# Transposing the adjacency of 64 small graphs: TensorE transposes against block loads and one VectorE transpose

## The chip, the cores and the metric

The kernel runs on one core of one Trainium2 chip. The metric is device microseconds of one execution; the median of three runs counts. The engines are named as in the profile: PE (TensorE), whose weight loads are listed as PEld, DVE (VectorE), ACT (ScalarE), POOL (GpSimd) and SP (SyncE), whose queue issues every DMA of this kernel.

## What is computed

Sixty-four independent graphs, each with 256 nodes and 512 features, pass through four graph layers. Every layer normalizes, clips at zero, mixes the nodes by a form of the adjacency, projects by a 512x512 weight (the last layer by 512x1024), and adds to the residual stream. All is float32.

```
h = max(layernorm(x), 0);  Wh = h @ W0
    e = leaky_relu(Wh @ a[:512] + (Wh @ a[512:])^T)
    x = x + elu(softmax(where(adj > 0.5, e, NEG_INF), axis=1) @ Wh)
h = max(layernorm(x), 0)
    Ah = adj + I;  d = rsqrt(rowsum(Ah));  x = x + relu((d * Ah * d^T) @ h @ W1 + bias)
h = max(layernorm(x), 0);  x = x + relu((adj @ h) @ W2) * mask
h = max(layernorm(x), 0);  agg = (adj @ h) / max(rowsum(adj), eps)
    x = x + relu(concat(h, agg) @ W3^T)
```

On TensorE the mixing products want the adjacency with its column index on the partitions, that is A^T. All four layers use it: layer 0 through its mask, layer 1 with the identity added, layers 2 and 3 as it is (in layer 3 scaled by the row sums).

## The kernel before

**One graph.** `graph(b)` describes the work of one graph as a list of operations, each with an engine, an estimated duration, a function that issues the instructions, and the tiles it reads and writes. It loads `xs` (the residual stream, two chunks of 128 nodes, line 353) and `a_nat` (the adjacency as it lies in memory, line 355). `transpose_a` (line 512) turns the four 128x128 quarters of `a_nat` on PE into a PSUM bank `pa`, and ACT copies the bank to `aT` in SBUF (line 522). DVE sums the rows of `a_nat` into `deg` (line 527), from which `dh` and `rdeg` follow.

Each layer then has the same frame. `norm` makes statistics (DVE), the scale (POOL) and `h` (ACT). `aggregate` (line 410) multiplies `h` with a moving matrix, in two halves `pt`: with `e` in layer 0 (the softmax, lines 546 to 581), `ahT` in layer 1 (`aT` plus identity, made by POOL, line 606), `aT` in layers 2 and 3. `left_sums` (line 396) brings the result out of PSUM in quarters and sums of quarters, and `project` (line 434) multiplies these by the weights with seven block products in place of eight (Winograd's scheme), in the PSUM banks `pz`, `py` and `pv`. DVE and ACT collect the results (`c`) and add them to `xs`. In layer 3 the product with `h` itself needs `h` transposed: DVE turns it in 32x32 blocks (`hb`, line 681), and 16 DMAs of 32 KB put each block to its place (`hw`, line 686). The result is stored from `xs` (line 701).

**The order.** No graph runs alone. `Plan` takes the operations of all graphs, with a due time that grows by `APART` = 14 for each graph, and `place` (line 69) goes through an imagined execution: each engine takes the operation that can start first, ties going to urgent ones and then to the earlier due time. `emit` writes the instructions out in the order of these starts, and this order is fixed for every engine, SP included. The estimates are multiplied by `STRETCH` except for PE and DMA; `SPARE` is added to the time at which a PE operation counts as ready. The plan's times only set the order: the instructions run as soon as what they need is there and the instruction before them on their engine has gone.

**Buffers.** Tiles share slots by tag. The number of slots of a tag is in `buffers` (line 713): five `xs` and five `aT`, one `a_nat`, four slots `mva` for `e` and `ahT`, one `off` for the mask (and, at the start, for the two halves of the vector a), and eight PSUM banks. A tile takes a slot once the one before has been read for the last time.

**Start.** `logit_weights` (line 256) multiplies W0 by the two halves of a, eight DVE operations (line 273) that the softmax of every graph waits for. `weight` and `last_weight` load the weights; POOL forms their block sums (line 293), and PE transposes W3 (line 329).

Of the kernel before, what the change touches and what calls it, by code (L numbers as in the profile page):

```python
# [14 lines left out]
P = 128  # L15
Q = 32
# [4 lines left out]
NEG_INF = -9000000000000000.0  # L21
HOP = 0.25
APART = 14.0
STRETCH = 1.12
SPARE = 0.0

# [12 lines left out]
class Plan:  # L41
# [9 lines left out]
        self.ops, self.writer, self.readers = [], {}, {}  # L51

    def add(self, eng, us, fn, reads, writes, tiles, due, urgent):
        if eng not in ("PE", "DMA"):
            us *= STRETCH
        op = Op(eng, us, fn, tiles, due, urgent)
        for k in reads:
            op.deps |= self.writer.get(k, set())
        for k in writes:
            op.deps |= self.writer.get(k, set()) | self.readers.get(k, set())  # L60
        for k in reads:
            self.readers.setdefault(k, set()).add(op)
        for k in writes:
            self.writer[k] = {op}
            self.readers[k] = set()
        self.ops.append(op)
        return op

    def place(self, buffers):
# [31 lines left out]
        for _ in self.ops:  # L101
            choice = None
            for eng, ops in waiting.items():
                here = None
                for op in ops:
# [3 lines left out]
                    ready = max(op.ready, got[0])  # L109
                    spare = SPARE if eng == "PE" else 0.0  # L110
                    rank = (max(free[eng], ready + spare), not op.urgent, op.due, op.at)
# [37 lines left out]
def kernel(  # L149
# [21 lines left out]
    nc = tc.nc  # L171
    B, N, F = x.shape
    O = w0.shape[1]
    NC = N // P
# [8 lines left out]
    ps = ctx.enter_context(tc.tile_pool(name="ps", bufs=1, space=PSUM))  # L183
# [4 lines left out]
    class Tiles:  # L188
# [5 lines left out]
        def declare(self, name, shape, pool=None, tag=None):  # L194
            tag = pool or tag or name
            self.tiles[name] = Buffered(shape, tag, f"{name}_{self.name}")
# [17 lines left out]
        def op(self, eng, us, fn, reads=(), writes=(), urgent=False):  # L214


            if eng == "DMA":
                us = 2.0 + us / 150.0
            named = [k.split(".")[0] for k in list(reads) + list(writes)]
            tiles = [self.tiles[n] for n in dict.fromkeys(named) if n in self.tiles]  # L220
            mine = lambda ks: [k if k[0] == "=" else (self.name, k) for k in ks]

            def go():
                self.open = tiles
                fn(self)

            plan.add(eng, us, go, mine(reads), mine(writes), tiles, self.due, urgent)


    ident = const.tile([P, P], F32, name="ident")  # L230
# [114 lines left out]
    def graph(b):  # L345

        me = Tiles(str(b), APART * b)
        op, declare, together = me.op, me.declare, me.together
# [85 lines left out]
        def project(operands, l, keep, keep_us, total, last, also=[]):  # L434
# [44 lines left out]
            snap("z", 0, 1)  # L479
            product("y", A12, B21, True)  # L480
            add("y", 0, 0)
            product("z", S3, T3, False)
            snap("z", 1, 1)
            add("v", 1, 1)
            product("z", A22, T4N, False)
            last(f"pz{l}")
            product("v", S4, B22, False)
            add("v", 0, 1)

        def plain_keep(i, j):  # L490
# [16 lines left out]
            )  # L507


        declare("pa", [P, NC, N], "ps")  # L510

        def transpose_a(g):
            for m in range(NC):
                for c in range(NC):
                    nc.tensor.transpose(  # L515
                        g["pa"][:, m, c * P : (c + 1) * P],
                        g["a_nat"][:, c, m * P : (m + 1) * P], ident
                    )

        op("PE", 0.45, transpose_a, ["a_nat", "=ident"], ["pa"])  # L520
        declare("aT", [P, NC, N])
        op("ACT", 0.59, lambda g: nc.scalar.copy(g["aT"], g["pa"]), ["pa"], ["aT"], urgent=True)
        declare("deg", [P, NC])
        declare("dh", [P, NC])
        declare("rdeg", [P, NC])
# [152 lines left out]

        declare("hb", [P, NC, F])
        for c in range(NC):  # L680
            op("DVE", 0.65, lambda g, c=c: nc.vector.transpose(g["hb"][:, c, :], g["h3"][:, c, :]),
               [f"h3.{c}"], [f"hb.{c}"])
        declare("hw", [P, 7, FH, P])
        parts = [(a, q) for a in range(P // Q) for q in range(P // Q)]
# [26 lines left out]
    for b in range(B):  # L711
        graph(b)
    buffers = dict(
        xs=5, a_nat=1, aT=5, h=4, mva=4, xw=4, hw=1, c=3, off=1, junk=4, b12=1, ex256=2, ex512=2,
        wa_col=1, hb=1, ps=8,
    )
    for tag in ("stats", "mv", "rstd", "nb", "deg", "dh", "rdeg", "lg", "top", "den", "mask"):
        buffers[tag] = 6
# [34 lines left out]
```

## Time and profile before

| what | value |
|---|---|
| median of three runs | 2949.46 us (2948.93 to 2951.12) |
| the profiled execution | 2949.19 us |
| its span, first to last instruction | 2947.4 us |
| mean granted TensorE clock | 0.997 |
| PE, pa matmuls (line 515) | 256 of 273 ns (median) |
| ACT, copy pa to aT (line 522) | 64 of 586 ns |
| DVE, transpose to hb (line 681) | 128 of 711 ns (median) |
| POOL, ahT (line 606) | 64 of 1291 ns |
| SP, one hw DMA issue (line 686) | 609 ns (median, 585 to 1905), 2.0 us to landing |
| SP, one a_nat issue (line 355) | 374 ns (median, 368 to 900), 2.7 us to landing |
| time of DMA packets | 17.1% of 16 engines' span, 335600 packets |

The span is measured by the profiler in one execution, and the 1.8 us between it and the time of the same execution lie around it. Busy times of PE overlap, as matmuls are pipelined: the mean duration of a 128x256 matmul is 379 ns, while 16 of them start within 3.45 us of each other. A float32 product of the code is two matmuls of the trace, so it occupies 0.43 us of the queue.

### The profile page before, as it was taken

What the parts mean: (1) busy time and instruction counts of PE and PEld (TensorE: products, weight loads), DVE (VectorE), ACT (ScalarE), POOL (GpSimd) and SP (SyncE); (2) the same over time, 40 slices, a digit from 0 to 9 for tenths busy, and PEclk for the clock granted to TensorE, in tenths of its full rate; (3) what the DMA queues carried; (4) which work ended last, traced back from release to release, by engine and by line L of the source; (5) the groups of instructions that cost most, each with busy time, mean ns of one, the idle gap of its engine ahead of it and who ended that gap; (6) DMA issues with size and microseconds to landing.
All of it is one profiled execution on the core that took longest, in us unless ns stands there. A gap on an engine that the chain in (4) does not pass through costs nothing.

```text
span 2947.4 us, 41121 instructions
## 1 busy us (share of the span) xinstructions
PE 2893.6 (98%) x13608; PEld 2536.1 (86%) x13608; DVE 2164.2 (73%) x5520; ACT 1364.4 (46%) x2899; POOL 1017.5 (35%) x1374
## 2 busy tenths in 40 slices
PE   5999999999999999999999999999999999999997
PEld 4888888888888888888888888888888888888886
DVE  8867777777777777777777777777777777777763
ACT  4544444444444444444444444444444444444432
POOL 6433333333333333333333333333333333333321
PEclk9999999999999999999999999999999999999999
DMA  4011111211211111111112111121121111121111
GB/s 146 15 34 50 44 37 39 51 36 40 50 30 47 47 33 47 42 38 47 37 40 51 36 40 49 31 48 46 34 47 38 39 50 36 40 51 30 43 29 36
DMA packets 335810, 127.21 MB, mean 43 GB/s; under 512 B 281968, under 2 KB 301424, under 8 KB 335600
## 3 DMA queue, kind: packets, MB, share of 16 engines
q1 hardware_dynamic: 335600, 124.60, 17.1%
q8 instruction: 109, 1.79, 0.3%
q14 instruction: 101, 0.83, 0.1%
HBM read 57.41 MB, written 33.55 MB: 31 GB/s over the span
## 4 chain that ended last, share of the span: by engine, by line
PE 97%; DVE 2%; SPq 1%; DMA 1%; issue 0%; ACT 0%; DVEq 0%
PE pz L451 37%; PE pt L420 30%; PE pv L451 19%; PE py L451 9%; PE pa L515 1%; SPq L686 1%; PE pl L240 0%; PE pr L240 0%; DMA a_l<-in_L_gnn_a_dram 0%; DVE junk_l L273 0%; DVE junk L541 0%; DVE e L565 0%; DVE e L563 0%; DMA hw<-hb 0%; DVE xs L595 0%
## 5 line engine op out<-in xcount | busy, mean ns | idle before, releaser
L451 PE MATMUL pz<-wb,xw 128*128 128x256 f32 x4096 | 992.7, 379 | 1.5 <-DVE c L611 1.2
L451 PEld LDWEIGHTS pz<-wb,xw 128*128 128x128 f32 x4096 | 773.4, 190 | 104.7 <-DVE c L611 1.4
L392 POOL TENSOR_TENSOR xw<-xw 128x256 f32<-128x256 f32 x512 | 418.5, 834 | 522.9 <-DVE xw L388 419.7
L451 PE MATMUL pv<-wb,xw 128*128 128x256 f32 x2048 | 525.5, 379 | 2.8 <-DVE c L493 2.8
L420 PE MATMUL pt<-aT,h 128*128 128x256 f32 x2048 | 473.4, 379 | 0.0
L420 PEld LDWEIGHTS pt<-aT,h 128*128 128x128 f32 x2048 | 389.1, 190 | 52.9
L451 PEld LDWEIGHTS pv<-wb,xw 128*128 128x128 f32 x2048 | 384.9, 190 | 53.3 <-issue 3.2
L491 ACT COPY c<-pz 128x256 f32<-128x256 f32 x576 | 214.5, 372 | 407.4 <-PE pz L451 392.2
L382 ACT ACTIVATE h<-xs,nb,rstd 128x512 f32<-128x512 f32 x512 | 390.2, 809 | 17.7 <-DVE nb L378 11.5
L371 POOL TENSOR_SCALAR rstd<-mv 128x2 f32<-128x2 f32 x256 | 127.7, 499 | 683.4 <-DVE mv L369 631.5
L367 DVE BATCH_NORM_STATS2 stats<-xs 128x6 f32<-128x512 f32 x512 | 333.2, 681 | 5.4 <-DMA xs<-in_x_dram 5.1
L493 DVE TENSOR_TENSOR c<-pv,c 128x256 f32<-128x256 f32 x384 | 161.8, 421 | 220.3 <-PE pv L451 171.5
L451 PE MATMUL pz<-wb,hw 128*128 128x256 f32 x1024 | 264.3, 381 | 10.8 <-DMA hw<-hb 9.6
L405 DVE TENSOR_TENSOR xw<-pt,xw 128x256 f32<-128x256 f32 x256 | 108.0, 422 | 225.0 <-ACT xw L400 224.9
L451 PE MATMUL py<-wb,xw 128*128 128x256 f32 x1024 | 263.1, 379 | 0.4 <-ACT xw L400 0.4
L392 POOL TENSOR_TENSOR hw<-hw 128x256 f32<-128x256 f32 x128 | 99.6, 781 | 436.3 <-DVE hw L388 418.3
L420 PE MATMUL pt<-e,h 128*128 128x256 f32 x1024 | 235.3, 383 | 11.2 <-DVE e L578 11.2
L400 ACT COPY xw<-pt 128x512 f32<-128x512 f32 x256 | 150.0, 586 | 189.8 <-PE pt L420 182.6
L420 PE MATMUL pt<-ahT,h 128*128 128x256 f32 x1024 | 232.2, 379 | 1.2 <-ACT h L382 1.2
L420 PEld LDWEIGHTS pt<-e,h 128*128 128x128 f32 x1024 | 196.4, 192 | 39.4 <-ACT h L382 8.9
L541 DVE SCALAR_TENSOR_TENSOR junk<-h,wa 128x512 f32<-128x512 f32 x256 | 228.2, 912 | 0.0
L451 PEld LDWEIGHTS pz<-wb,hw 128*128 128x128 f32 x1024 | 190.0, 191 | 35.8 <-issue 10.4
(90 smaller groups left out, 3552.5 us busy)
## 6 DMA issues: line engine op xcount, KB each, us to landing
xs<-in_x_dram SPq DMA_DIRECT2D x64, 512.0 KB, 4.2
hw<-hb SPq DMA_DIRECT2D x1024, 32.0 KB, 2.0
out_dram<-xs SPq DMA_DIRECT2D x64, 512.0 KB, 2.8
a_nat<-in_adj_dram SPq DMA_DIRECT2D x64, 256.0 KB, 2.7
w3n_w<-in_L_gnn_W_dram SPq DMA_DIRECT2D x4, 512.0 KB, 4.3
wb<-in_L_gnn_kernel_dram SPq DMA_DIRECT2D x6, 256.0 KB, 7.0
w_l<-in_L_gnn_W_dram SPq DMA_DIRECT2D x4, 256.0 KB, 6.8
wb<-in_L_gnn_W_dram SPq DMA_DIRECT2D x3, 256.0 KB, 3.9
```

The lines of the kernel that those rows point to most:

```text
L367: op("DVE", 0.69, lambda g, c=c: nc.vector.bn_stats(g[st][:, c, :], g["xs"][:, c, :]), XS[2 * c : 2 * c + 2], [f"{st}.{c}"])
L371: op("POOL", 0.31, lambda g: nc.gpsimd.tensor_scalar_add(g[rs], g[mv][:, :, 1], EPS_LN), [f"{mv}.0", f"{mv}.1"], [rs])
L382: op("ACT", 0.81, lambda g, c=c: nc.scalar.activation(g[h][:, c, :], g["xs"][:, c, :], AF.Relu, bias=g[nb][:, c : c + 1], scale=g[rs][:, c ...
L392: op("POOL", 0.85, lambda g, i=i, o=o: nc.gpsimd.tensor_tensor(g[xw][:, o], g[xw][:, i], g[xw][:, S2], ALU.subtract), put(i, S2), put(o), ...
L400: op("ACT", 0.59, lambda g: nc.scalar.copy(g[xw][:, A12 : A22 + 1 : A22 - A12].rearrange("p h k n -> p k h n"), g[hi].rearrange("p k (h n) ...
L405: op("DVE", 0.43, lambda g: nc.vector.tensor_tensor(g[xw][:, S1], g[lo][:, :, P:], g[xw][:, A22], ALU.add), [lo] + put(A22), put(S1), urge ...
L420: nc.tensor.matmul(g[pt][:, kk, :], lhsT=g[h][:, c, k * P : (k + 1) * P], rhs=g[moving][:, c, :], start=(c == 0), stop=(c == NC - 1),)
L451: nc.tensor.matmul(g[t], lhsT=g[xw][:, left, k], rhs=wb[n_w][:, right, k], start=start and at == 0, stop=at == ends, skip_group_check=True,)
L491: return "ACT", lambda g, to, block: nc.scalar.copy(to, block)
L493: plain_total = (0.43, lambda g, i, to, block: nc.vector.tensor_tensor(to, block, to, ALU.add))
L515: nc.tensor.transpose(g["pa"][:, m, c * P : (c + 1) * P], g["a_nat"][:, c, m * P : (m + 1) * P], ident)
L541: op("DVE", 0.77, lambda g, j=j, c=c: nc.vector.scalar_tensor_tensor(g[f"junk{j}{c}"], g["h0"][:, c, :], 1.0, wa[:, j, :], ALU.mult, ALU.mult,
```

## The change

The adjacency is loaded twice. `a_nat` stays, for the row sums. Beside it, eight DMAs of 32 KB bring the same matrix into a new tile `ab`, in 32x32 blocks: each block is put where its transpose belongs in A^T, but itself not turned. One DVE instruction then turns all 64 blocks in place of their positions and writes `aT`. The PE transposes, the PSUM bank `pa` and the ACT copy are gone. Each DMA moves runs of 32 floats, 128 bytes, 256 of them.

Along with this the planner's constants and the slots change: `STRETCH` becomes a factor for each engine (DVE 1.1, ACT 1.15, POOL 1.06, before 1.12 for all three), `SPARE` goes from 0 to 0.15, the estimate of the hb transpose from 0.65 to 0.71, and the slots are xs 6 (5), mva 3 (4), off 2 (1), ex256 3 (2), ex512 1 (2) and a new tag ab with 1. So the order of all engines is planned anew.

```diff
-STRETCH = 1.12
-SPARE = 0.0
+STRETCH = {"DVE": 1.1, "ACT": 1.15, "POOL": 1.06, "PE": 1.0, "DMA": 1.0}
+SPARE = 0.15
...
-        if eng not in ("PE", "DMA"):
-            us *= STRETCH
+        us *= STRETCH[eng]
...
-        declare("pa", [P, NC, N], "ps")
-
-        def transpose_a(g):
-            for m in range(NC):
-                for c in range(NC):
-                    nc.tensor.transpose(
-                        g["pa"][:, m, c * P : (c + 1) * P],
-                        g["a_nat"][:, c, m * P : (m + 1) * P], ident
-                    )
-
-        op("PE", 0.45, transpose_a, ["a_nat", "=ident"], ["pa"])
+        declare("ab", [P, NC, N], tag="ab")
         declare("aT", [P, NC, N])
-        op("ACT", 0.59, lambda g: nc.scalar.copy(g["aT"], g["pa"]), ["pa"], ["aT"], urgent=True)
+        for q in range(P // Q):
+            rows = adj[b].rearrange("(i r) (c q j) -> q r c i j", r=Q, c=NC, j=Q)[q]
+            for c in range(NC):
+                op("DMA", 32, lambda g, q=q, c=c, rows=rows: nc.sync.dma_start(
+                    g["ab"][q * Q : (q + 1) * Q, c, :].rearrange("r (i j) -> r i j", j=Q),
+                    rows[:, c]), (), [f"ab.{q}{c}"])
+        op("DVE", 0.7, lambda g: nc.vector.transpose(g["aT"], g["ab"]),
+           [f"ab.{q}{c}" for q in range(P // Q) for c in range(NC)], ["aT"])
...
-            op("DVE", 0.65, lambda g, c=c: nc.vector.transpose(g["hb"][:, c, :], g["h3"][:, c, :]),
+            op("DVE", 0.71, lambda g, c=c: nc.vector.transpose(g["hb"][:, c, :], g["h3"][:, c, :]),
...
     buffers = dict(
-        xs=5, a_nat=1, aT=5, h=4, mva=4, xw=4, hw=1, c=3, off=1, junk=4, b12=1, ex256=2, ex512=2,
-        wa_col=1, hb=1, ps=8,
+        xs=6, a_nat=1, ab=1, aT=5, h=4, mva=3, xw=4, hw=1, c=3, off=2, junk=4, b12=1, ex256=3,
+        ex512=1, wa_col=1, hb=1, ps=8,
     )
```

## The prediction, made before the changed kernel had run

> **What bounds the kernel now.** I read, in this order: busy shares and slices of the page, the chain that ended last (shares, then its pieces in order of time), one stretch of TensorE's timeline, the busy time of the transposes (tile pa) by stretch, and TensorE's waits.
>
> ```profile
> PE 2893.6 (98%) x13608; PEld 2536.1 (86%) x13608; DVE 2164.2 (73%) x5520; ACT 1364.4 (46%) x2899; POOL 1017.5 (35%) x1374
> ...
> PE   5999999999999999999999999999999999999997
> ...
> DVE  8867777777777777777777777777777777777763
> ...
> PE 97%; DVE 2%; SPq 1%; DMA 1%; issue 0%; ACT 0%; DVEq 0%
> ```
>
> TensorE is full in every slice but the first and the last, and 97% of the chain runs on it; in the first slice DVE is the fuller one (8 against 5). Pieces of the chain, start and length in us, each the first 16 instructions of one period:
>
> ```profile
> 2672.55 3.45 PE pt L420 x16
> ...
> 2717.46 3.45 PE pt L420 x16
> ...
> 2762.38 3.45 PE pt L420 x16
> ...
> 2806.85 3.45 PE pt L420 x16
> ```
>
> The chain repeats per graph: 44.91, 44.92, then 44.47 us. The last period is the first in which no adjacency is transposed (the last pa matmul starts at 2760.4). So the trace itself holds a period without the removed work: 0.45 us shorter. The timeline agrees:
>
> ```profile
> 1502.54 0.60 PE L515 MATMUL pa<-ident,a_nat 128*128 128x128 f32 x4
> 1502.98 1.03 PE L451 MATMUL pz<-wb,hw 128*128 128x256 f32 x4
> ```
>
> The next matmul starts 0.44 us after pa began, with no idle bracket at either. Where pa stands (stretch; TensorE busy, instructions; weight load; ACT or clock):
>
> ```profile
> 0.00:92.00 92.00, 3.98 (x20) 3.05 (x20) 2.91 (x5) 0.98 0.37 120
> 92.00:350.00 258.00, 3.00 (x20) 2.44 (x20) 2.95 (x5) 1.00 0.15 35
> 350.00:2800.00 2450.00, 32.40 (x216) 26.96 (x216) 31.66 (x54) 1.00 0.17 42
> ```
>
> Five graphs' transposes fall into the fill (0 to 92 us), where TensorE waits anyway; 5 + 54 = 59 stand in the full part. TensorE's own waits sum to 36 us before 92, 2.2 us from 92 to 2800 and 10.3 us after (hw DMAs at the end). The largest of the fill:
>
> ```profile
> PE pt L420 <- DVE e L578: 10.8, 2, 8.6
> PE pw_l L240 <- DVE mv L369: 9.7, 1, 9.7
> ```
>
> The fill is set by DVE, at whose end the first product starts, at 33.73 us.
>
> **What the Trainium skill says.** "VectorE: DVE Perf Modes", The three transpose paths: DVE turns only independent 32x32 blocks and writes SBUF, TensorE turns 128x128 into PSUM. So the blocks must be loaded in their final grid. The trace agrees in kind: hb is turned by DVE in blocks at 711 ns for 128x512. "DMA: Bandwidth & Descriptors", Why small descriptors are slow (HBM only): short runs from HBM pay a fixed overhead each. The hw copies have 128-byte runs but go SBUF to SBUF, so no row here shows it. "SBUF — State Buffer", Who interferes with whom: DVE and GpSimd share a port pair that one holds alone. In the trace DVE's L565 takes 1.64 to 1.68 us beside a busy POOL in the first 50 us and 0.69 later, while the 128 block transposes stay within 668 and 715 ns: the added operation is of the kind that isn't slowed.
>
> **The change, part by part.**
>
> TensorE: 4 transposes a graph go, 0.44 us of the queue. In the full part 59 x 0.44 = 26.0 us come off the end; the five in the fill bring nothing.
>
> ACT: 64 copies of 586 ns go (37.5 us). ACT is 46% busy and ends no wait of weight on the chain: nothing. The PSUM bank of pa goes too; no TensorE wait for it is seen: nothing.
>
> DVE: 64 x 0.71 = 45 us come. From 350 to 2800 us DVE is busy 1817.7 of 2450 us, 33.3 us of a period; after, 34.0 of 44.47 (76%). Its idle time there ends mostly on TensorE, which hides the addition. If that cover were gone, it would cost 0.71 x 59 = 42 us at most, nothing at least. In the order of the changed program's instructions I followed the tightest point: the second half of e (L576) is preceded on DVE by the sums of pv, pz, py of layers 1 and 2. From the end of the pz of layer 1 DVE has hw's sum, one c sum, L576 and the pz sum itself, about 0.48 + 0.42 + 0.42 + 0.35, with hops about 2.1 us; TensorE has 9 products of 0.432 us = 3.9 us before it needs e. Slack 1.8 us. The pr to pt distance of layer 3 stays 8 products, 3.5 us, with about 2.3 us spare. I take nothing.
>
> The new wait: the transpose needs eight DMAs. In steady state ab is filled right after the previous graph's transpose, a period early, so DVE isn't held; behind it would stand off, deg and the logit sums.
>
> SP: 8 issues a graph. Nearest row: hw, also 32 KB in 256 runs of 128 bytes, 609 ns each and 2.0 us to landing; so 4.9 us of SP, plus a_nat's 0.37. SP's order becomes ab x8, a_nat, hw x16, out, xs; the x load leaves hw's midst. ab waits for the transpose, hw for the second hb transpose, 17 DVE instructions and about 8 us later: 8 - 5.3 = 2.7 us to spare. hw needs 16 x 0.61 + 2.0 = 11.8 us; between hb and the first product on hw TensorE has about 50 products and 4 small ones, 22.0 us: 10.2 us more. Cost nothing at 609 ns; the bound below is given by the slower rival. DMA engines go from 17% to an estimated 23% (131072 more packets beside 335600): hidden. a_nat runs up to seven graphs ahead, freed by deg alone, and the output is written at the same place in the cycle.
>
> Costs of the planner (STRETCH, SPARE) and buffers: xs 6 and off 2 loosen, mva 3 and ex512 1 tighten. ahT now waits on POOL for a buffer that is released by TensorE (e's or ahT's second half of pt); POOL's next sums of xw are wanted 46 products (20 us) after that release. Between nothing and 0.3 us a period (18 us); I take nothing.
>
> Fill: both a0 halves are loaded at the start (off 2), so the eight L273 sums run in one go from 8.9 us at 0.62 each, to 13.8 instead of 21.2. From there 12.5 us lay to the first product; add about 1.3 for h, which was ready before and isn't now, 0.7 for the transpose, 1.2 for two statistics. That gives 29.5 instead of 33.7: 4.2 us. The third graph's first product (82.4 us) has about the same DVE work ahead of it: three more transposes (2.1 us) and a second pair of statistics against one deg, four rdeg and the fifth graph's statistics. I take 3.5 us. Bounds: 12 us gained (the second graph's e could be 10 us earlier), 16 lost (36 us of waits growing by less than half, if the added DMAs, packets and w3n loads behind ab come late).
>
> End: the order from the last pt of layer 2 is the same but for one product: nothing.
>
> Sum: span 2947.4 - 26.0 - 3.5 = 2917.9; the profiled execution took 2949.19, 1.8 more than its span, so 2919.7. It stands 0.3 under the median 2949.46: 2920.
>
> **Rivals.**
>
> A, the forecast: 2920 (own range 2911 to 2929), chance 0.60.
>
> B, the fill gets longer: DVE is its bound and gets transposes, and the SP queue puts 8 issues of 4.9 us before the second x and the layer-1 weights, with waits for the transposes among them. For it: the 8 against 5 in slice one. Against: the earlier L273. 26 gained, 12 to 16 lost, or small TensorE gaps of 0.3 us a period: 2930 to 2941, centre 2936. Chance 0.23.
>
> C, the fill gains much: second graph 10 us earlier and kept: 2909 or less. Chance 0.08.
>
> D, no change: the shorter TensorE period isn't reached, since a producer chain (DVE or ACT) opens a gap as long as pa was: 2944 to 2949. Against: the period of 44.47 in the trace, on the same engines' work. Chance 0.04.
>
> E, slower: SP. If reading runs of 128 bytes makes each ab issue take over 2.2 us, the eight and a_nat (18 us) use up their 5.3 and the 2.7 + 10.2 us of slack, and hw comes late for its product. At 2.4 us (a hw issue of 1.9 us occurs): 19.2 + 0.4 - 18.2 = 1.4 us a period, 58 periods, 81 us: 3001. For it: reads from HBM unmeasured here; against: all a_nat issues with 256 runs took 0.37 to 0.9 us. Chance 0.05.
>
> **How the numbers follow.** The likeliest is A, 2920. Below the range lies most of C, above it D, E and the upper end of B: 2909 to 2938. About 0.2% (6 us) is what a measurement can tell from no change; faster, under 2943.6: A, B and C, 0.91; same 0.04; slower 0.05.
>
> **What would show it.** Right: no L515 and L522; pt of layer 0 returning every 44.47 us; TensorE waits between 92 and 2800 still a few us; DVE 76% with 64 transposes of 0.71 us; ab issues near 0.61 us; first product near 29.5 us. Wrong: a gap before the products on hw (E), waits on DVE e, xw or POOL ahT repeating each period (D), or the 92 us mark reached late (B).

## The result and the profile after

The changed kernel takes 2918.99 us (median of four executions, 2918.09 to 2919.62), the kernel before, run beside it, 2949.19 (2948.67 to 2951.12). The ratio is 0.9896, its 95% interval 0.9879 to 0.9913: about 1% faster. The profiled execution took 2918.48 us, its span is 2916.7, and its granted clock 0.997 as before. The span is 30.7 us shorter.

First the page of the changed kernel: busy times, the slices of TensorE and VectorE, the chain that ended last.

```profile
PE 2865.8 (98%) x13352; PEld 2515.4 (86%) x13352; DVE 2244.1 (77%) x5584; ACT 1292.8 (44%) x2835; POOL 1014.0 (35%) x1374
...
PE   5999999999999999999999999999999999999997
...
DVE  8877877777777777777777777777777777878753
...
PE 97%; DVE 1%; DMA 1%; SPq 0%; ACT 0%; issue 0%; POOL 0%; POOLq 0%
```

256 TensorE instructions are gone (64 graphs with 4 transposes each), and still TensorE is full in the same slices and holds 97% of the chain. What bounds the kernel hasn't changed; there is less of it. The pieces of the chain, in order of time, show how much less:

```profile
2678.17 3.45 PE pt L420 x16
...
2722.65 3.45 PE pt L420 x16
...
2767.12 3.45 PE pt L420 x16
```

The first product of a graph returns after 44.48 and 44.47 us, where it took 44.91: exactly the period that the trace of before showed once, at its end. TensorE's waits after the first 92 us (microseconds in all, times, longest) are this one line up to 2800 us, and these after it:

```profile
PE pt L420 <- ACT h L382: 3.3, 1, 3.3
```

```profile
PE pz L451 <- DMA hw<-hb: 8.2, 1, 8.2
PE pz L451 <- ACT c L491: 1.2, 3, 0.5
PE pz L451 <- issue: 0.7, 1, 0.7
```

3.3 us against 2.2 before, and 10.1 against 10.3 at the end. So the full part has no new gap. The new loads and the new transpose, by their tile:

```profile
L516 SPq DMA_DIRECT2D ab<-in_adj_dram x512: 311/448/1829, 4.6 to 2690.7; - x171
L519 DVE STREAM_TRANSPOSE aT<-ab x64: 671/677/712, 15.8 to 2731.1; 128x512 f32<-128x512 f32 x64
...
DMA to landing us min/median/max: 1.6/1.9/7.1
```

Minimum, median and maximum in ns, then the first and last start. In the median an issue costs SP 448 ns and its data have landed 1.9 us after the issue began; the transpose takes 677 ns and never more than 712. The start of the timeline of TensorE's products holds what is left of the difference (the bracket is the idle time before, and what ended it):

```profile
28.55 6.08 PE L420 MATMUL pt<-e,h 128*128 128x256 f32 x16 [10.94 <-DVE e L576]
...
43.95 0.67 PE L420 MATMUL pt<-e,h 128*128 128x256 f32 x2 [1.34 <-DVE e L576]
48.50 5.92 PE L420 MATMUL pt<-e,h 128*128 128x256 f32 x14 [3.88 <-DVE e L576]
54.26 1.03 PE L451 MATMUL pz<-wb,xw 128*128 128x256 f32 x4
```

The first product starts at 28.55 us, 5.2 us earlier than before. The gain of the span is 30.7 us: 59 x 0.44 = 26.0 from the full part, and 4.7 that are left for the start (called the fill). So not quite the whole of the earlier first product reaches the end.

TensorE's own account says more. All its waits add up to 48.7 us in the kernel before (36.2 up to 92 us, 2.2 up to 2800, 10.3 after) and to 45.9 in the changed one (32.5, 3.3, 10.1), which is 2.8 less. The other 27.9 us of the gain are nearly the transposes of all 64 graphs, 64 x 0.44 = 28.2. So about 2 of the 4.7 us are the transposes of the five graphs in the start, which the prediction put at nothing, and the rest is less waiting. This is an account of what happened, and doesn't say what each cause would have brought alone.

### The profile page after: what moved, and what is told of

Read it like the earlier page. It is cut to its first block, busy times and chain, and to the rows that moved or that the text cites. A ratio compares the mean times of both kernels' runs of the same rounds, so it can differ in the third digit from the quotient of the medians.

```text
span 2916.7 us, 40926 instructions
## 1 busy us (share of the span) xinstructions
PE 2865.8 (98%) x13352; PEld 2515.4 (86%) x13352; DVE 2244.1 (77%) x5584; ACT 1292.8 (44%) x2835; POOL 1014.0 (35%) x1374
## 2 busy tenths in 40 slices
DMA packets 475075, 144.01 MB, mean 49 GB/s; under 512 B 421232, under 2 KB 440688, under 8 KB 474864
## 3 DMA queue, kind: packets, MB, share of 16 engines
q1 hardware_dynamic: 474864, 141.41, 20.3%
q8 instruction: 107, 1.75, 0.3%
## 4 chain that ended last, share of the span: by engine, by line
PE 97%; DVE 1%; DMA 1%; SPq 0%; ACT 0%; issue 0%; POOL 0%; POOLq 0%
PE pz L451 38%; PE pt L420 30%; PE pv L451 19%; PE py L451 9%; PE pr L240 0%; PE pl L240 0%; SPq L684 0%; DMA w_l<-in_L_gnn_W_dram 0%; POOL wb L293 0%; DMA wb<-in_L_gnn_W_dram 0%; DMA wb<-in_L_gnn_kernel_dram 0%; DVE xs L590 0%; DMA w3n_w<-in_L_gnn_W_dram 0%; DVE e L576 0%; DVE stats L367 0%
## 5 line engine op out<-in xcount | busy, mean ns | idle before, releaser
L451 PE MATMUL pv<-wb,xw 128*128 128x256 f32 x2048 | 515.8, 379 | 0.0
L382 ACT ACTIVATE h<-xs,nb,rstd 128x512 f32<-128x512 f32 x512 | 396.5, 811 | 4.7 <-DVE nb L378 4.6
L539 DVE SCALAR_TENSOR_TENSOR junk<-h,wa 128x512 f32<-128x512 f32 x256 | 211.5, 847 | 67.6 <-ACT h L382 67.5
L420 PE MATMUL pt<-e,h 128*128 128x256 f32 x1024 | 237.2, 386 | 17.2 <-DVE e L576 17.2
L420 PE MATMUL pt<-ahT,h 128*128 128x256 f32 x1024 | 242.9, 381 | 3.3 <-ACT h L382 3.3
L420 PEld LDWEIGHTS pt<-ahT,h 128*128 128x128 f32 x1024 | 195.9, 191 | 30.6 <-ACT h L382 4.1
L451 PEld LDWEIGHTS py<-wb,xw 128*128 128x128 f32 x1024 | 194.6, 190 | 26.4 <-ACT xw L400 0.4
L403 ACT COPY xw<-pt 128x256 f32<-128x256 f32 x256 | 95.3, 372 | 248.3 <-PE pt L420 247.5
```

Of the source, the lines that this page charges most:

```text
L382: op("ACT", 0.81, lambda g, c=c: nc.scalar.activation(g[h][:, c, :], g["xs"][:, c, :], AF.Relu, bias=g[nb][:, c : c + 1], scale=g[rs][:, c ...
L403: op("ACT", 0.38, lambda g: nc.scalar.copy(g[xw][:, A11], g[lo][:, :, :P]), [lo], put(A11), urgent=True)
L420: nc.tensor.matmul(g[pt][:, kk, :], lhsT=g[h][:, c, k * P : (k + 1) * P], rhs=g[moving][:, c, :], start=(c == 0), stop=(c == NC - 1),)
L451: nc.tensor.matmul(g[t], lhsT=g[xw][:, left, k], rhs=wb[n_w][:, right, k], start=start and at == 0, stop=at == ends, skip_group_check=True,)
L539: op("DVE", 0.77, lambda g, j=j, c=c: nc.vector.scalar_tensor_tensor(g[f"junk{j}{c}"], g["h0"][:, c, :], 1.0, wa[:, j, :], ALU.mult, ALU.mult,
```

## The experiments

In what follows, "fill effect" is the difference of a run's span to the span of before (2947.4), with the 26.0 us of the full part added back where the PE transposes are gone: -4.7 for the changed kernel. It rests on one profiled execution of each kernel, and the medians of the kernel before differ by up to 0.9 us from one experiment to another, so 1 us of it means nothing.

**The new path alone.** The changed kernel with the planner constants and the slots of before, and one slot `ab`.

```diff
-STRETCH = {"DVE": 1.1, "ACT": 1.15, "POOL": 1.06, "PE": 1.0, "DMA": 1.0}
-SPARE = 0.15
+STRETCH = {"DVE": 1.12, "ACT": 1.12, "POOL": 1.12, "PE": 1.0, "DMA": 1.0}
+SPARE = 0.0
...
-        xs=6, a_nat=1, ab=1, aT=5, h=4, mva=3, xw=4, hw=1, c=3, off=2, junk=4, b12=1, ex256=3,
-        ex512=1, wa_col=1, hb=1, ps=8,
+        xs=5, a_nat=1, ab=1, aT=5, h=4, mva=4, xw=4, hw=1, c=3, off=1, junk=4, b12=1, ex256=2, ex512=2,
+        wa_col=1, hb=1, ps=8,
```

(The hb estimate also goes back to 0.65.)

> The new path of the adjacency (block loads, one DVE transpose) with the planner's constants and the slots of the kernel before (one slot of ab added). Theory (TensorE's queue is the sum, the plan only moves the fill): every period 0.44 us shorter, 44.47 us, 26 to 28 us off, the fill as before since off has one slot and the second half of a is loaded late again: 2921 to 2925 us. Rival (the new constants and slots are needed to turn the removed work into time, as without them a producer's wait opens in every period): periods above 44.6 us and 2935 us or more.

Measured: 2922.96 us (2922.59 to 2923.22), ratio 0.9909 (0.9895 to 0.9922), span 2921.4, period 44.47. So the path alone gives the 26.0 us of the full part, and a fill effect of 0.0. TensorE's waits (46.9 us) are only 1.0 us more than in the changed kernel; what is left of the span without them is 2874.5 us against 2870.8, for the same matmuls. So they ran 3.7 us slower, and the last section shows the lower clock that goes with it. One thing didn't fit: with one slot `off` its first product nevertheless started at 31.18 us, well before the 33.73 of the kernel before.

**The plan alone.** The kernel before, PE transposes and all, with the new constants, slots and hb estimate.

```diff
-STRETCH = 1.12
-SPARE = 0.0
+STRETCH = {"DVE": 1.1, "ACT": 1.15, "POOL": 1.06, "PE": 1.0, "DMA": 1.0}
+SPARE = 0.15
...
-        xs=5, a_nat=1, aT=5, h=4, mva=4, xw=4, hw=1, c=3, off=1, junk=4, b12=1, ex256=2, ex512=2,
+        xs=6, a_nat=1, aT=5, h=4, mva=3, xw=4, hw=1, c=3, off=2, junk=4, b12=1, ex256=3, ex512=1,
```

> The new constants and slots with the TensorE transposes and the ACT copy of before. Theory: the period stays at 44.91 us, only the fill gets shorter, by 3 to 5 us: 2944 to 2947 us. Rival (the plan carries the gain): 2930 us or less. Third way (three slots for e and ahT and one of ex512 are too few once pa takes a PSUM bank again): gaps in each period, 2955 us or more.

Measured: 2952.89 us (median of 13 executions, which lie far apart: 2946.81 to 2955.58), ratio 1.0004 (0.9995 to 1.0012). The period stays 44.91, so the rival in which the plan carries the gain is out. The third way is out too, as TensorE doesn't wait at all from 350 to 2780 us. The expected gain of the fill was missed: by itself the plan is worth between 3 us gained and 5 us lost, from one execution to the next. In the profiled execution (one of the longer, 2954.43 us) the first product starts early, at 30.57 us, and TensorE waits 48.1 us, hardly less than the 48.7 of before; but its matmuls take 5 us more (span without waits 2903.9 against 2898.7). From 80.1 to 86.9 us its granted clock is 0.50, where the kernel before has 1.00. Whether the clock also explains the shorter executions isn't shown, as none of them was traced.

**One slot off.** This undoes one item of the change, the one on which the forecast of the fill rested.

```diff
-        xs=6, a_nat=1, ab=1, aT=5, h=4, mva=3, xw=4, hw=1, c=3, off=2, junk=4, b12=1, ex256=3,
+        xs=6, a_nat=1, ab=1, aT=5, h=4, mva=3, xw=4, hw=1, c=3, off=1, junk=4, b12=1, ex256=3,
```

> The changed kernel with one slot of off in place of two, so the second half of a can only be loaded after the first four sums of L273. Theory: the first product of layer 0 starts 3 to 5 us later than 28.55 us (32 to 34 us) and the time is 2921 to 2924 us, with the period at 44.47 us. Rival (the first product's start doesn't decide the fill, since later waits take up what it loses): first product late by 3 us or more, and yet 2919 us within 1 us.

Measured: 2916.22 us (2915.65 to 2917.0), ratio 0.9886 (0.9873 to 0.9900). It is faster than the changed kernel, so the theory falls; and it is faster than the rival allowed too. TensorE's products in its start:

```profile
30.50 5.93 PE L420 MATMUL pt<-e,h 128*128 128x256 f32 x16 [11.58 <-DVE e L576]
...
47.57 5.38 PE L420 MATMUL pt<-e,h 128*128 128x256 f32 x16 [3.23 <-DVE e L576]
52.78 1.03 PE L451 MATMUL pz<-wb,xw 128*128 128x256 f32 x4
```

The first product is 2 us later than in the changed kernel, the end 2.7 us earlier. So two slots `off` do bring the first product forward, but that isn't what decides the length of the fill. The second graph's product stands in one piece here and is done by 52.78 us, where the changed kernel splits it (43.95 and 48.50) and is done by 54.26. TensorE's waits for `e` up to 92 us, in the changed kernel and then with one slot:

```profile
PE pt L420 <- DVE e L576: 17.2, 4, 10.9
```

```profile
PE pt L420 <- DVE e L576: 14.8, 2, 11.6
```

These 2.4 us are nearly the whole difference of 2.7, and by 350 us TensorE has executed 17 matmuls more than in the changed kernel (1454 against 1437). Why the order with one slot has `e` of the later graphs ready sooner isn't shown. Both kernels were run again, this time side by side:

> The changed kernel itself, beside the version with one slot off on the same chip. Theory (one slot off is better by what its start gains, 2.7 us by spans): 2918 to 2920. Rival (the difference between the two earlier runs is the chip's): both within 1 us of each other.

> The changed kernel with off=1 in place of off=2, beside the changed kernel on the same chip. Theory: 2915.5 to 2917, 2 to 4 us below it, its executions all below those of the changed kernel. Rival: within 1 us of it.

Measured: 2918.29 us (2917.45 to 2920.07) for the changed kernel, 2915.52 (2915.00 to 2915.98) with one slot; ratios to before 0.9893 (0.9876 to 0.9909) and 0.9884 (0.9869 to 0.9899). No execution of the one is among those of the other, and the medians lie 2.8 us apart. The first products start at 29.71 and 31.32 us here: the start of one and the same kernel moves by about 1 us between executions. With one slot it is the fastest version found.

**Why the first product came earlier at all.** In the kernel before, the last four of the eight sums on L273 ran beside GpSimd's first weight sums (L293, from 15.6 us on). The first of the four, which began before them at 15.2 us, took 0.99 us, the other three 1.74 to 1.75 each. These are the instructions of L273 in the kernel before and then in the changed one:

```profile
L273 DVE SCALAR_TENSOR_TENSOR junk_l<-w_l,a_l x8: 657/842/1746, 8.9 to 19.5; 128x512 f32<-128x512 f32 x8
```

```profile
L273 DVE SCALAR_TENSOR_TENSOR junk_l<-w_l,a_l x8: 658/687/693, 8.7 to 13.2; 128x512 f32<-128x512 f32 x8
```

In the changed kernel SP's eight `ab` issues stand ahead of the weight loads, so the weights come later. To test the collision by itself, the kernel before got one more dependency in its planner that puts these weight sums later in GpSimd's order, and nothing else.

```diff
-               [key(i), key(j)], [key(to)])
+               [key(i), key(j)] + (["=wa1"] if n == 0 else []), [key(to)])
```

> The kernel before (PE transposes, old constants and slots), in which the order puts GpSimd's first weight sums (L293) behind the second ahT, by one more dependency of the planner; nothing else is edited, though the order of the start changes with it. Theory (the first product came earlier in the changed kernel because the weight loads stand behind the ab issues, so that GpSimd's sums no longer run beside the L273 sums): all eight L273 sums take 0.66 to 0.71 us (in before the last four took up to 1.75), and the first product starts at 28.5 to 31.5 us in place of 33.73. The period stays 44.91. What the earlier first product is worth at the end is a separate question: by the runs so far, between 0 and 4 us, so 2944 to 2950. Rival (the collision is not the cause): some L273 sums still take over 1.2 us, or they take 0.7 us and the first product stays later than 32.5 us.

Measured: 2947.27 us (20 executions, 2945.12 to 2949.19), ratio 0.9990 (0.9983 to 0.9997).

```profile
L273 DVE SCALAR_TENSOR_TENSOR junk_l<-w_l,a_l x8: 660/689/694, 8.8 to 17.8; 128x512 f32<-128x512 f32 x8
```

With GpSimd out of the way all eight sums take 0.69 us, though the transposes are still on PE and there is still one slot `off`. The first product starts at 31.81 us, 0.3 us outside what was expected and 1.9 earlier than before; at the end 1.6 us of span are won (2.5 by the medians of that occasion). So the collision costs about 2 us of the first product, and one slot in place of two about 2 more (28.55 against 30.50; 1.6 in the second pair). Of the 5.2 us by which the first product came earlier, about 1 us is left without a cause, no more than it moves between executions. The path alone fits in: with its `ab` issues ahead of the weights its eight sums take 0.73 us at most, and its first product starts at 31.18 us, near the 31.81 here.

**How much room VectorE has.** The transpose is issued twice, then six times, with the same source and the same destination; nothing else is changed.

```diff
-        op("DVE", 0.7, lambda g: nc.vector.transpose(g["aT"], g["ab"]),
+        op("DVE", 0.7, lambda g: [nc.vector.transpose(g["aT"], g["ab"]) for _ in range(2)],
```

> The changed kernel with the DVE transpose done twice, one behind the other, in the same place of the same order; 64 x 0.62 to 0.68 = 40 to 44 us more of DVE, busy 79%. Theory (the DVE transpose is hidden behind TensorE in the full part): the period stays 44.47 us, only the four or five transposes of the fill show: 2919 to 2922 us. Rival (DVE stands on TensorE's path, and the first transpose already cost part of the gain): 0.3 to 0.6 us a period, 2937 to 2958 us.

Measured: 2920.04 us (2919.18 to 2920.70), ratio 0.9898 (0.9883 to 0.9913): 1 us more than the changed kernel, for some 43 us of additional transposes. The kernel before was 0.9 us slower on that occasion as well, so the second transpose costs next to nothing.

> The changed kernel with the DVE transpose done six times in its place: 5 x 0.62 = 3.1 us more of DVE in every period, busy about 84%, and everything behind it on DVE (off, deg, the logit sums, L405 and L388 of layer 1) 3.1 us later. Theory (cover by slack, the tightest point of the order has about 2 us, but not behind the transpose, and DVE's idle time of 10 us a period takes the rest up): full part at 44.47 us or up to 0.3 us above, the fill 3.1 us longer for each of three or four graphs: 2928 to 2950 us. Rival (DVE's slack was nearly used up by one transpose): 1.5 to 3.1 us in every period, 3010 to 3110 us.

Measured: 2936.86 us (2934.97 to 2938.35), ratio 0.9958 (0.9941 to 0.9974). Busy times of this kernel from 350 to 2780 us (length; PE, PEld, DVE, ACT, POOL; clock, DMA share, GB/s):

```profile
350.00:2780.00 2430.00, 2430.00 (x11368) 2136.25 (x11367) 2113.16 (x5017) 1094.16 (x2401) 847.79 (x1135) 1.00 0.20 48
```

With VectorE at 87% TensorE still has no gap in the full part. Five more transposes for each graph cost 18 us, 16.2 by the spans. All of it lies in the start, where TensorE's waits grow from 32.5 to 41.9 us before 92 us, and from 3.3 to 7.9 up to 350 us; the other 2 us are slower matmuls after these waits. So the added transpose is hidden with a wide margin in the full part, and is paid where VectorE sets the pace.

**How much room SP has.** Each of the eight loads is cut into four, then into eight, with the same bytes in the same places: 32 and 64 issues for each graph.

```diff
-                op("DMA", 32, lambda g, q=q, c=c, rows=rows: nc.sync.dma_start(
-                    g["ab"][q * Q : (q + 1) * Q, c, :].rearrange("r (i j) -> r i j", j=Q),
-                    rows[:, c]), (), [f"ab.{q}{c}"])
+                op("DMA", 32, lambda g, q=q, c=c, rows=rows: [nc.sync.dma_start(
+                    g["ab"][q * Q : (q + 1) * Q, c, i * Q : (i + 2) * Q].rearrange("r (i j) -> r i j", j=Q),
+                    rows[:, c, i : i + 2]) for i in range(0, 8, 2)], (), [f"ab.{q}{c}"])
```

> The changed kernel with each of the eight block loads of a graph cut into four (32 DMAs of 8 KB in the same order, same bytes and runs): at the 0.31 to 0.37 us of the shortest issues seen, 10 to 12 us of SP in place of 3.6. Theory (SP has about 2.7 + 10.2 us of slack before hw comes late, counted over 5.3 us of issues, 18 us in all): periods stay 44.47 us, 2919 to 2923 us with a longer fill. Rival (SP was already close to delaying hw): waits for hw of 4 us or more a period, 3150 us or more.

Measured: 2959.96 us (2957.83 to 2961.87), ratio 1.0035 (1.0022 to 1.0048), slower than before. A smaller piece isn't a cheaper issue: 425 ns in the median, so 32 of them take SP about 15 us where 10 to 12 had been expected. Still hw isn't late; from 600 us on TensorE never waits until the end, where it does in the changed kernel too. Its busy time in stretches of this kernel, columns as above:

```profile
0.00:150.00 150.00, 92.94 (x387) 75.73 (x388) 101.49 (x237) 55.50 (x125) 68.39 (x81) 0.94 0.31 89
...
350.00:600.00 250.00, 242.83 (x1112) 212.06 (x1111) 185.13 (x471) 109.57 (x240) 85.01 (x118) 0.98 0.20 46
600.00:1000.00 400.00, 400.00 (x1873) 351.65 (x1872) 311.68 (x784) 180.14 (x397) 139.02 (x190) 1.00 0.21 48
```

The theory was right on the full part and missed the total: the fill is 37 us longer than in before (span 2958.0, less 2947.4, plus 26.0). There weights, `xs` and blocks come through the one queue: four of the transposes alone wait 25.2 us for their blocks.

> As the run with 32, but 64 DMAs of 4 KB a graph: at 0.31 to 0.37 us each 20 to 24 us of SP behind the transpose. Theory (18 us in all are free): hw comes 2 to 6 us late in every period, TensorE waits for DMA hw, 58 periods: 3030 to 3270 us. Rival (more slack than counted, as SP and hw can lag by a part of a period without meeting a product): still within 2919 to 2935 us.

Measured: 3809.85 us (3808.11 to 3810.68), ratio 1.2915 (1.2895 to 1.2934). Two consecutive views of one period of this kernel, first SP's queue, then TensorE:

```profile
2003.35 30.92 SPq L516 DMA_DIRECT2D ab<-in_adj_dram x64
2034.37 0.39 SPq L355 DMA_DIRECT2D a_nat<-in_adj_dram x1
2034.93 10.41 SPq L684 DMA_DIRECT2D hw<-hb x16
```

```profile
2047.15 2.05 PE L451 MATMUL pz<-wb,hw 128*128 128x256 f32 x4 [11.10 <-DMA hw<-hb]
2048.99 1.91 PE L451 MATMUL pz<-wb,xw 128*128 128x256 f32 x4
2050.70 1.63 PE L451 MATMUL pv<-wb,xw 128*128 128x256 f32 x4
```

The hw loads stand behind 31 us of issues, and TensorE waits 11.1 us for them here. From 700 us on it has 52 such waits, 557 us in all, and hardly another. This is the mechanism of the slower rival, made large. The period is 58.16 us: 44.47, the wait of 11.1, and some 2.4 more because the twelve matmuls after the wait take 5.0 us until the next begins in place of 2.6. The time lies far above the 3030 to 3270 expected for three reasons: an issue costs 419 ns however small it is, the matmuls after each wait are slow, and before 700 us TensorE waits another 210 us or so in the longer start.

The same places in the changed kernel, SP's queue:

```profile
2020.28 4.77 SPq L516 DMA_DIRECT2D ab<-in_adj_dram x8
2025.14 0.40 SPq L355 DMA_DIRECT2D a_nat<-in_adj_dram x1
2036.43 10.39 SPq L684 DMA_DIRECT2D hw<-hb x16
```

After a_nat SP is idle for 10.9 us. What it waits for before hw, from the queue's waits of this kernel:

```profile
SPq L684 <- DVE hb L679: 446.7, 56, 23.0
SPq L684 <- PE pz L451: 279.9, 62, 12.1
```

First for hb, and then in 62 of 64 graphs for TensorE too: until the last product has read the one slot of hw. The last of the 16 issues begins at 2046.22, so the loads have landed at about 2048.1 (1.9 us later), and the first product on hw starts at 2052.82: 4.7 us after that. So SP's room is 10.9 + 4.7 = 15.6 us beyond the 5.3 that it uses in this period. The 64 issues take 26.2 us more, and 26.2 - 15.6 = 10.6 is near the 11.1 seen; with 64 issues the product starts some 0.5 us after the last landing, which makes up the difference.

**Two more transposes out of TensorE's queue.** By the same reasoning the spreading of the inverted row sums (`pr`, two PE transposes for each graph, 0.22 us) could go: two small DMAs through DRAM write them to all partitions. (The cut leaves out the declaration of the DRAM tiles, their two slots, and the smaller operand of the product with `aT`.)

```diff
-        declare("pr", [P, N], "ps")
-
-        def spread_rdeg(g):
-            for c in range(NC):
-                spread(g["pr"][:, c * P : (c + 1) * P], g["rdeg"][:, c : c + 1])
-
-        op("PE", 0.23, spread_rdeg, ["rdeg", "mv3.0", "=ident"], ["pr"])
+        declare("rd", [NC, P], tag="rd")
+        declare("pr", [P, F], tag="junk")
+        op("DMA", 1, lambda g: nc.sync.dma_start(
+            g["rd"].rearrange("c p -> p c"), g["rdeg"]), ["rdeg", "mv3.0"], ["rd"])
+        op("DMA", 128, lambda g: nc.sync.dma_start(
+            g["pr"][:, :N], g["rd"].rearrange("(u c) p -> u (c p)", u=1).to_broadcast([P, N])), ["rd"], ["pr"])
```

> The changed kernel with another small work taken from TensorE: the row pr of layer 3 (rdeg spread over all partitions, two transposes, 0.22 us of the queue) is made by two DMAs through a scratch row in DRAM, one out and one back spread over the partitions. Theory (in the full part time is TensorE's queue, whatever leaves it comes off): 44.25 us a period, 59 x 0.22 = 13 us: 2903 to 2909 us. Rival (the second DMA's wait for the first, 2 us or more, stands on SP's queue before hw or the x load): gaps that eat it, 2918 us or more.

Measured: 2929.02 us (2926.64 to 2932.89), ratio 0.9931 (0.9916 to 0.9946): faster than before, slower than the changed kernel. The period is 44.25, as worked out, so the full part did save its 13 us, and the theory still missed the total by 20 us. Against the changed kernel TensorE waits 7.5 us more up to 350 us and 8.1 us more at the end, and its matmuls are slower by another 6 to 7 us. The second attempt adds one slot `off`, to mend the start:

> The changed kernel with the row sums spread over the partitions by two small DMAs through DRAM in place of two PE transposes per graph (as in the earlier run, which had a period of 44.25 and a gapless full part, but a longer start and end), and with one slot off. Theory (the period saves 0.22 us a graph, 13 us over the full part, and the loss lay in the start's order, which one slot off makes as good as in the run with one slot off alone): 2903 to 2912. Rival (the DMAs wait in SP's queue ahead of the ab and hw issues and lengthen start and end whatever the order): 2922 to 2932.

Measured: 2934.17 us (2931.32 to 2936.53), ratio 0.9946 (0.9931 to 0.9961). The order of the start didn't mend it, as the rival had it, and the time lies 2 us above even the rival's range. Its last graph, pieces of the chain in order of time:

```profile
2876.48 0.97 DVE xs L658
2877.77 9.25 DMA rd<-rdeg
2887.03 3.63 DMA pr<-rd
2891.26 3.64 PE pt L423 x8
```

(Line 423 here is line 420 of the changed kernel.) 1 KB in runs of 4 bytes takes 9.25 us to land, and the broadcast of it 3.6 more. While other graphs fill TensorE this is hidden. At the end little is left to hide it: 14.8 us from the last addition to `xs` (L658) to the product, a place at which the changed kernel's TensorE doesn't wait. The hw loads come later in turn: TensorE waits 13.9 us for them here, 8.2 in the changed kernel. Meanwhile SP stands waiting for the first DMA before it can issue the second, 64 times, 434.7 us in all.

## Why the prediction was right, by its steps

**TensorE, 26.0 us: right.** The period of 44.47 us and the absence of new gaps show it in the trace, and the path alone gave just this.

**ACT and the PSUM bank, nothing: not contradicted.** ACT's share fell from 46% to 44% and no TensorE wait of the full part moved. It wasn't tried by itself.

**VectorE, hidden: right.** One transpose more costs at most 1 us, five more leave the full part without a gap. The forecast of 76% for the stretch from 350 to 2800 us came out as 78% (1905.0 us of 2450). The transposes there are 36.6 us, 0.68 each. Some operations became slower in the new order: `nb` (L378) takes 63.7 us there in place of 31.9, the sum of hw (L689) 39.0 in place of 23.4. That they now lie beside GpSimd is an inference, not shown.

**SP, 5.3 us with 12.9 to spare: right in what it decides, wrong inside.** An issue took 448 ns in the median, not the 609 taken from hw. Eight and a_nat took 5.3 us in the period shown all the same, as one of the eight took 1.43 us there; in the median of the full part the eight take 3.8. The prediction took hw to start when the second hb transpose has gone and gave 2.7 us before it and 10.2 behind. In fact that transpose comes later, and the one hw slot is freed by TensorE later still: 10.9 us before, 4.7 behind. The sum, 15.6, is near the 12.9 predicted because the two errors have opposite signs. So the bound at which the slower rival begins (18 us of issues in the prediction, some 20 as measured) stood: 15.5 us of issues didn't make hw late, 31.3 did.

**DMA engines at an estimated 23%: 20.3%.** The packets came nearly as counted (474864 against 335600 + 131072 = 466672; what the 8192 more are isn't shown). The short runs from HBM landed in 1.9 us, as the hw copies of the same size within SBUF did. So the overhead for each run, for which the prediction had named the Trainium skill, "DMA: Bandwidth & Descriptors", Why small descriptors are slow (HBM only), isn't to be seen in the landing time at 32 KB.

**The planner and the slots, nothing in the full part: right.** The plan alone left the period at 44.91.

**The fill, 3.5 us: the size was near (4.7), and its reason is the step that failed.** The prediction had the eight L273 sums run in one go because two slots `off` let both halves of a be loaded at once, and carried the earlier first product to the end. The first half is so in part: the sums do end at 13.9 us, and the slots are worth about 2 us of the first product; but another 2 us came from a collision with GpSimd that the later weights took away. The prediction counted 0.62 us for each sum without asking why three of them had taken 1.74 us. The second half is wrong: the version with one slot has a later first product and an earlier end. What differs there is how long the second and third graph wait for `e` (17.2 us in all waits for `e` against 14.8). Against the path alone it is something for which the prediction had no term: nearly the same waits, but matmuls that take 3.7 us longer. And the transposes of the five graphs in the start, put at nothing, make up about 2 of the 4.7 us in TensorE's account. That the size agreed is luck.

**The end, nothing: right** (10.1 against 10.3 us).

Of the rivals, B (a longer fill) and E (hw late) are real mechanisms that this change doesn't reach: more transposes or more issues bring them about. C (2909 us or less) didn't come. D is out by the period.

## What to carry to other kernels

Where one engine is full, what leaves its queue comes off the time one to one, as long as no new wait opens; a period of the same trace without that work is the best sign of it. What is added elsewhere is free only as far as the wait that ends last there leaves room, and that room is found by looking at which semaphore really releases the queue (here a buffer slot, not the producer). The start and the end of a pipelined kernel have other bounds than its middle: a path with long latency can win in every period and lose it all there. An earlier first product says little of when the start is over; the matmuls done by a fixed later time say more.

## What the hardware showed that was not expected

After a long wait matmuls are slow for a while. In the changed kernel 16 of them take 5.92 us to the start of the next instruction after a wait of 10.94, where they take 3.45 later on. The 14 after the wait of 3.88 take 5.76 in place of 3.0. With 64 issues a period each wait of 11.1 us costs 2.4 us more. For the 14 the granted clock shows it (the third number from the end, 0.50; it is 1.00 from 54 us on):

```profile
47.10:53.80 6.70, 5.30 (x13) 4.23 (x14) 5.78 (x15) 1.08 (x2) 4.16 (x8) 0.50 0.21 42
```

For the 16 the same view gives 1.00 (28.5 to 33.3 us), though the matmuls run at half their pace; there the lower clock is an inference. The Trainium skill, "TensorE: Matmul & The Clock Gate", Part 1: The HAM clock gate, says that TensorE falls to half its clock after an idle window of about 3.4 us and needs about as long under load to return. The trace agrees on the half, and in size on the time: under load from 48.50 us, the clock is 0.50 up to 53.8. But a single wait of that length isn't needed. With the path alone the clock fell after three waits of 1.0, 0.3 and 1.5 us in the 7 us before:

```profile
58.80:65.50 6.70, 6.15 (x15) 4.46 (x14) 5.74 (x13) 3.10 (x7) 0.93 (x2) 0.50 0.34 119
```

So short waits close together can cost more than their own length, and two orders with nearly the same waits can differ by some microseconds, as these two runs do (3.7 us).

Beside GpSimd's weight sums, VectorE's sums of L273 took 1.75 us in place of 0.69, while all 64 block transposes of the changed kernel stay between 671 and 712 ns. Among them is one that lies wholly beside such a weight sum (at 85.9 us, 711 ns). The Trainium skill, "SBUF — State Buffer", Who interferes with whom, names a pair of ports that VectorE and GpSimd share and that one holds alone; the run with the late sums shows the effect on L273 go away when GpSimd's sums are moved. That it is the ports, no run shows.

An `ab` issue on SP costs 419, 425 and 448 ns (medians) for 4, 8 and 32 KB, so cutting a load multiplies the cost. A DMA of 256 runs of 4 bytes to DRAM takes 9.2 us (median) to land, against 1.9 for 256 runs of 128 bytes from DRAM; whether the direction or the length of the runs makes the difference wasn't tried.
